# Residual adds by transfer, row-wise mixing of one column of weights, and a later statistic, at the start of the second layer of a deformable convolution and a mixture-of-experts convolution

## The chip, the core and the metric

The kernel runs on one core of one Trainium2 chip. A core has five engines that each work through their own queue in order: TensorE (PE; its weight loads are listed as PEld), VectorE (DVE), ScalarE (ACT), GpSimd (POOL) and SyncE (SP), which here only issues DMA transfers. POOL issues transfers too, from a queue of its own. All of them share 16 DMA engines. Matrix products go to PSUM, everything else lives in SBUF. The metric is the time of one execution on the device, in microseconds.

## What is computed

Two layers on eight images of 128 channels and 64 x 64 pixels, in float32. Both layers have a residual, and both normalise their input per group of four channels first. Cut to what matters here:

```python
# layer 0: deformable convolution, batch norm over all images, relu
y = deform_conv(group_norm(x), off_w, off_b, w, b)
x = x + relu((y - mean(y)) * rsqrt(var(y) + 1e-5) * gamma + beta)
# layer 1: mixture of four 3x3 convolutions, two chosen per image
g = group_norm(x)
scores = sigmoid(mean(g, (2, 3)) @ gate_w.T + gate_b)
wd = dense(top2(scores + gate_bias), scores)      # (8, 4), sums to 1 per image
x = x + sum_e wd[:, e] * conv3x3(g, expert_w[e]) + conv3x3(g, shared_w) + biases
```

The convolution is linear in its weights, so the kernel mixes the four experts and the shared weights into one set per image, and adds the residual as a multiple of the identity in the middle tap.

## The kernel before

`dense()` is layer 0: it samples, convolves and writes the raw result of each image to DRAM (`ydram`), with statistics for the batch norm. It ends at about 1043 us of the profile. `layer1()` then takes one image after another.

**Preparing an image** is a generator, `prepare(b, made)`. Its `yield`s are the places where it hands back control, and so set where its instructions land in each engine's queue. It has these steps:

1. Batch norm, relu and residual. For image 0 this goes over eight chunks `c` of 512 pixels per channel (lines 1410 to 1421): a relu on ACT (line 1415) in place in `x1`, an add of `xt0`, the input that was loaded ahead, by POOL for even chunks and by VectorE for odd ones (line 1417), and, two chunks later, the chunk's statistics on VectorE (`bn_stats`, line 1419). For the other images it goes over four quarters: a relu (line 1426) and a transfer from DRAM, issued by POOL, that adds the input onto `x1` as it lands (line 1429). Their statistics are on line 1437.
2. The group statistics: aggregate (line 1440), a small product with a grouping matrix for the mean (`pm`, line 1444), small operations on VectorE (`d`, `e`, `gm`), a second product for the variance (`pv`, line 1454), and a power on POOL (line 118) for the scale. For image 1 seven `yield`s stand ahead of `pm`, and one ahead of `pv`.
3. The gate: a product (`pg`, line 1476), a sigmoid, and a ranking on VectorE that gives the mixing weights `wd`. Between these ACT normalises the image into `pad2` in eight chunks (line 1467).
4. Mixing. `wmix` holds the mixed weights by row, column, output. Each of its columns `kx` is the shared weights plus four expert terms, one VectorE operation per expert (line 1546). From `wmix` come `u1` and `u2` (lines 1557 to 1561), since the convolution saves products by working on pairs of rows: product `j` is 0 with row 0 of the weights, 1 with `u1`, 2 with `u2`, 3 with row 2. `transform(g, which, engine)` (lines 1525 to 1529) makes the matching inputs `v` of block `g` from `pad2`: `which` 1 for product 1, `which` 2 for product 2, `which` 0 for products 0 and 3. For image 0 the three columns are mixed one after the other and the transforms of the first block stand between them; for the other images all columns are mixed at once.

**The products** of an image: four blocks `g` of 16 rows, in each the products `j` in the order 1, 2, 0, 3, in each three columns `kx` (line 1618). Only in image 0's first block does the loop over columns stand outside that over `j`, so that products can begin when column 0 is mixed. After each `j` a `collect` is put into the queues: ACT for `j` 1, VectorE for the others. Also after each `j`, the preparation of the next image goes on by two steps (three after `j` 3), and for image 0 its own remaining transforms by one.

**Transfers around the change.** SP's queue, in order: the last stores of layer 0, five small gate tensors, the shared weights `sw_sb` and the four experts' `ew_sb` (576 KB each, lines 1397 and 1399), image 1 (four of 512 KB, line 1379), then image 2 into the buffer of image 0 once that is normalised. Image 0 and its input are loaded while layer 0 still runs.

The instructions that only run under `tc.If` at the end of the program (a general form of layer 0, and layer 1 once more) do not run here.

Of the kernel before, what the change touches and what calls it, by code (L numbers as in the profile page):

```python
# [11 lines left out]
ALU = mybir.AluOpType  # L12
# [17 lines left out]
NE = 4  # L30
# [35 lines left out]
def deform_moe_conv(  # L66
# [18 lines left out]
    nc = tc.nc  # L85
# [10 lines left out]
        out=gsel, in_=gsel, compare_op=ALU.is_ge, fill=0.0, base=0,  # L96
# [3 lines left out]
        out=gsel, in_=gsel, compare_op=ALU.is_ge, fill=0.0, base=3,  # L100
# [1237 lines left out]
    def layer1():  # L1338
# [6 lines left out]
        with ExitStack() as st:  # L1345
# [59 lines left out]
            def prepare(b, made):  # L1405
# [4 lines left out]
                if b == 0:  # L1410
                    for c in range(NCH + 2):
                        if c < NCH:
                            part = slice(c * CH, (c + 1) * CH)
                            y = x1[:, part]
                            nc.scalar.activation(y, y, AF.Relu, bias=yshift, scale=yscale)
                            adder = nc.gpsimd if c % 2 == 0 else nc.vector
                            adder.tensor_tensor(y, y, xt0[:, part], ALU.add)
                        if c > 1:
                            nc.vector.bn_stats(
                                stats[:, c - 2, :], x1[:, (c - 2) * CH : (c - 1) * CH]  # L1420
                            )
                else:

                    for q in range(4):
                        part = slice(q * HW // 4, (q + 1) * HW // 4)
                        nc.scalar.activation(
                            x1[:, part], x1[:, part], AF.Relu, bias=yshift, scale=yscale
                        )
                        nc.gpsimd.dma_start(
                            out=x1[:, part], in_=x[b, :, part], accum_op=ALU.add  # L1430
                        )
                        if b > 1:
                            yield
                    if b > 1:
                        yield
                    for c in range(NCH):
                        nc.vector.bn_stats(stats[:, c, :], x1[:, c * CH : (c + 1) * CH])
                        yield
# [10 lines left out]
                nc.vector.scalar_tensor_tensor(ev, d, d, mv[:, 1:2], ALU.mult, ALU.add)  # L1449
                gm = small.tile([P, 1], F32, name="gm")  # L1450
                nc.vector.tensor_tensor(gm, mv[:, 0:1], d, ALU.subtract)
                yield
                pv = ps_s.tile([P, 4], F32, name="pv", tag="pss")
                nc.tensor.matmul(pv[:, 0:1], lhsT=gsel, rhs=ev, start=True, stop=True)
                yield
# [10 lines left out]
                def normalise(c):  # L1466
                    nc.scalar.activation(
                        pad2[:, 1 + 8 * c : 9 + 8 * c, 1 : W + 1],
                        x1[:, c * CH : (c + 1) * CH].rearrange("p (h w) -> p h w", w=W),
                        AF.Identity, bias=shift, scale=scale,  # L1470
                    )
# [48 lines left out]
                def transform(g, which, engine):  # L1520
                    v, r = vs[g], 2 * TR * g
                    even = pad2[:, r + 2 : r + 2 * TR + 2 : 2]
                    odd = pad2[:, r + 1 : r + 2 * TR + 1 : 2]
                    if which == 1:
                        engine.tensor_tensor(v[:, 2 * TR : 3 * TR], odd, even, ALU.add)  # L1525
                    elif which == 2:
                        engine.tensor_tensor(v[:, 3 * TR :], even, odd, ALU.subtract)
                    else:
                        engine.tensor_tensor(
                            v[:, 0 : 2 * TR], pad2[:, r : r + 2 * TR],  # L1530
                            pad2[:, r + 2 : r + 2 * TR + 2], ALU.subtract,
                        )
# [9 lines left out]

                for kx in range(3) if b == 0 else (slice(0, 3),):
                    part = wmix[:, :, kx]
                    for e in range(NE):
                        nc.vector.scalar_tensor_tensor(
                            part, experts[:, e, :, kx], wd[:, e : e + 1],
                            part if e else shared[:, :, kx], ALU.mult, ALU.add,
                        )
                        if b:  # L1550
                            normalise(4 + e)
                            yield
                    if b or kx == 1:
                        nc.vector.scalar_tensor_tensor(
                            wmix[:, 1, 1], ident, inv, wmix[:, 1, 1], ALU.mult, ALU.add
                        )
                    nc.vector.tensor_tensor(u2[:, kx], part[:, 0], part[:, 2], ALU.add)
                    nc.vector.tensor_tensor(u1[:, kx], u2[:, kx], part[:, 1], ALU.add)
                    if kx == 0:
                        transform(0, 1, nc.vector)  # L1560
                    nc.vector.tensor_tensor(u2[:, kx], u2[:, kx], part[:, 1], ALU.subtract)
                    if kx == 0:
                        transform(0, 2, nc.vector)
                        transform(0, 0, nc.vector)
                    yield
                if b == 0:
                    mix_biases()
# [16 lines left out]
            for b in range(B):  # L1584
                load(b + 2)
                ahead_of = prepare(b + 1, made) if b + 1 < B else iter(())
                vs, us, bmix = made.pop(b)
                for g in range(NG):
                    yo = b2.tile([P, TR, 2, W], F32, name="yo")
                    part = {}  # L1590

                    def collect(j, pc, g=g, b=b, yo=yo, part=part, bmix=bmix):

                        if j == 1:
                            part["t"] = b2.tile([P, TR, W], F32, name="t1")
                            nc.scalar.activation(part["t"], pc, AF.Identity, bias=bmix, scale=0.5)  # L1596
                        elif j == 2:
                            for name, sign in (("s", 0.5), ("d", -0.5)):
                                part[name] = b2.tile([P, TR, W], F32, name=name + "12")
                                nc.vector.scalar_tensor_tensor(  # L1600
                                    part[name], pc, sign, part["t"], ALU.mult, ALU.add
                                )
                        elif j == 0:
                            nc.vector.tensor_tensor(yo[:, :, 0], pc, part["s"], ALU.add)
                        else:
                            nc.vector.tensor_tensor(yo[:, :, 1], part["d"], pc, ALU.subtract)
                            n = 2 * TR * W
                            nc.sync.dma_start(
                                out=out[b, :, g * n : (g + 1) * n],
                                in_=yo.rearrange("p t i w -> p (t i w)"),  # L1610
                            )

                    def product(j, kx, pc):
                        rows = {
                            0: slice(0, 2 * TR, 2), 1: slice(2 * TR, 3 * TR),
                            2: slice(3 * TR, 4 * TR), 3: slice(1, 2 * TR, 2),
                        }[j]
                        nc.tensor.matmul(  # L1618
                            pc, lhsT=us[j][:, kx], rhs=vs[g][:, rows, kx : kx + W],
                            start=(kx == 0), stop=(kx == 2),  # L1620
                        )

                    order = (1, 2, 0, 3)
                    pcs = {}
                    if b == g == 0:

                        pcs = {j: ps_m.tile([P, TR, W], F32, name="pc") for j in order}
                        for kx in range(3):
                            for j in order:
                                product(j, kx, pcs[j])  # L1630
                    for j in order:
                        pc = pcs.get(j)
                        if pc is None:
                            pc = ps_m.tile([P, TR, W], F32, name="pc")
                            for kx in range(3):
                                product(j, kx, pc)
                        todo.append((collect, j, pc))
                        if len(todo) > 1:
                            f, *args = todo.pop(0)
                            f(*args)  # L1640
                        if b == 0:
                            next(first, None)
                        for _ in range(3 if j == 3 else 2):
                            next(ahead_of, None)
                for _ in ahead_of:
                    pass
# [59 lines left out]
```

## Time and profile before

| what | us |
|---|---|
| three runs | 1418.2, 1424.83, 1427.55; median 1424.83 |
| the profiled execution | 1419.31 |
| its span, first to last instruction | 1417.3 |
| TensorE busy in the span | 1290.2 (91%) |
| VectorE busy | 1063.5 (75%) |
| ScalarE busy | 834.3 (59%) |
| POOL busy | 477.6 (34%) |

The span by stage. The columns are the busy time of PE and of VectorE, the TensorE clock that was granted as a share of the full one, and what the DMA engines moved:

| stretch, us | what | PE | DVE | clock | GB/s |
|---|---|---|---|---|---|
| 0 to 50 | start of layer 0 | 17.59 | 30.58 | 0.86 | 120 |
| 50 to 1010 | layer 0 | 899.88 of 960 | 738.88 | 0.97 | 186 |
| 1010 to 1043 | end of layer 0 | 31.55 of 33 | 6.37 | 1.00 | 23 |
| 1043 to 1067 | batch norm, image 0 prepared | 1.99 of 24 | 17.26 | 0.58 | 259 |
| 1067 to 1113 | products of image 0, image 1 prepared | 43.67 of 46 | 41.28 | 0.96 | 121 |
| 1113 to 1417 | images 1 to 7 | 295.49 of 304 | 229.16 | 1.00 | 124 |

An engine's busy time matters in a stage where it is close to the stage's length. A wait is told with what released it: "[2.33 <-DVE e L1449]" behind an instruction says that its engine stood idle for 2.33 us until VectorE's operation of line 1449 had written `e`.

### The profile page before, as it was taken

How to read it: one execution, taken by the hardware profiler on the slowest of the kernel's cores; microseconds unless marked ns; L12 is line 12 of the kernel's file. 1: busy time of each engine (PE TensorE's matmuls, PEld its weight loads, DVE VectorE, ACT ScalarE, POOL GpSimd, SP SyncE). 2: the span in 40 equal slices, each digit the busy share in tenths (PEclk: the TensorE clock that was granted, in tenths of full speed). 3: DMA queues.
4: the chain of work that ended last, by engine and by line, in shares of the span. 5: the costliest groups of instructions: out<-in, count | busy, mean ns of one | idle time of the engine just before them, and what ended most of it. 6: DMA issues, size and time to landing. Idle time of an engine off the chain costs nothing.

```text
span 1417.3 us, 21259 instructions
## 1 busy us (share of the span) xinstructions
PE 1290.2 (91%) x7561; PEld 731.6 (52%) x7561; DVE 1063.5 (75%) x2124; ACT 834.3 (59%) x1110; POOL 477.6 (34%) x748
## 2 busy tenths in 40 slices
PE   4169889999999999999999999999948999999998
PEld 1144456555656655655565565666623444444443
DVE  5757868689788878968978886756448987778972
ACT  2365856886787688688679768767522333222220
POOL 6444044534425543452552554354021010001000
PEclk9579989999999999999999999999978999999999
DMA  4589686977978887897887887799245654456411
GB/s 145 114 192 206 137 182 157 213 182 171 210 181 180 194 195 175 180 207 184 193 210 183 179 207 159 159 228 220 66 160 147 163 146 123 127 153 178 104 57 51
DMA packets 149430, 234.55 MB, mean 165 GB/s; under 512 B 101677, under 2 KB 104890, under 8 KB 139074
## 3 DMA queue, kind: packets, MB, share of 16 engines
q0 software_dynamic: 79248, 136.19, 44.4%
q1 hardware_dynamic: 69522, 96.37, 24.2%
q8 instruction: 61, 1.00, 0.3%
q10 hardware_dynamic: 544, 0.54, 0.1%
q14 instruction: 55, 0.45, 0.1%
HBM read 180.23 MB, written 45.35 MB: 159 GB/s over the span
## 4 chain that ended last, share of the span: by engine, by line
PE 57%; DMA 12%; ACT 12%; issue 8%; DVE 6%; POOL 3%; SPq 2%; DVEq 0%; ACTq 0%; POOLq 0%
PE py L934 21%; PE pc L1618 17%; PE pq L884 11%; DMA ywts<-taby 3%; PE pc L456 3%; PE pt L825 3%; ACT xwts L776 2%; DMA combo<-colwise 2%; ACT work L638 2%; DMA pad<-in_x_dram 1%; ACT samples L894 1%; DMA x<-in_x_dram 1%; DVE s L868 1%; POOL ywts L738 1%; ACT xt L841 1%
## 5 line engine op out<-in xcount | busy, mean ns | idle before, releaser
L934 PE MATMUL py<-samples,dw_sb 128*128 128x512 f32 (+3 forms) x1296 | 555.1, 561 | 9.7 <-ACT y L942 9.7
L738 POOL DMA_DIRECT2D ywts<-taby x510 | 335.0, 671 | 368.0 <-DMA xwts<-tabx 151.8
L934 PEld LDWEIGHTS py<-samples,dw_sb 128*128 128x128 f32 x1296 | 226.8, 189 | 206.8 <-issue 174.2
L884 PE MATMUL pq<-s,xt 64*128 64x144 f32 (+1 forms) x3840 | 284.4, 302 | 29.8 <-ACT samples L894 22.5
L884 PEld LDWEIGHTS pq<-s,xt 64*128 64x128 f32 x3840 | 257.6, 191 | 78.6 <-ACT samples L894 26.9
L894 ACT COPY samples<-pq 128x864 f32<-128x864 f32 (+1 forms) x318 | 278.5, 973 | 27.2 <-PE pq L884 27.1
L868 DVE TENSOR_TENSOR s<-xwts,ywts 128x432 f32<-128x432 f32 (+1 forms) x448 | 199.0, 498 | 49.5 <-PE pq L884 45.4
L1618 PE MATMUL pc<-v,u 128*128 128x512 f32 x384 | 174.3, 600 | 6.3 <-DVE v L1525 6.3
L1618 PE MATMUL pc<-v,wmix 128*128 128x512 f32 x384 | 173.2, 596 | 0.0
L776 ACT ACTIVATE xwts<-xwts,place 128x1152 f32<-128x1152 f32 (+3 forms) x132 | 153.1, 1164 | 7.9 <-DMA xwts<-tabx 7.9
L782 DVE TENSOR_SCALAR xwts<-xwts 128x1152 f32<-128x1152 f32 (+2 forms) x128 | 96.0, 751 | 80.4 <-ACT xwts L776 75.3
L1596 ACT ACTIVATE t<-pc,bmix 128x512 f32<-128x512 f32 x32 | 22.0, 687 | 187.5 <-PE pc L1618 98.8
L757 POOL DMA_DIRECT2D xwts<-tabx x126 | 73.5, 590 | 164.3 <-DVE samples L911 34.9
L1618 PEld LDWEIGHTS pc<-v,u 128*128 128x128 f32 x384 | 71.8, 191 | 92.9 <-issue 83.1
L1618 PEld LDWEIGHTS pc<-v,wmix 128*128 128x128 f32 x384 | 72.0, 189 | 90.9 <-issue 88.9
L942 ACT ACTIVATE y<-py,db_sb 128x512 f32<-128x512 f32 (+3 forms) x72 | 45.8, 636 | 118.0 <-PE py L934 110.8
L828 ACT COPY xt<-pt 128x512 f32<-128x512 f32 x126 | 73.9, 587 | 61.0 <-PE pt L825 51.4
L825 PEld LDWEIGHTS pt<-ident,picked 128*128 128x128 f32 x504 | 59.0, 142 | 92.5 <-ACT xt L828 41.8
L825 PE MATMUL pt<-ident,picked 128*128 128x128 f32 x504 | 78.1, 278 | 23.5 <-DVE picked L791 17.0
L791 DVE COPY picked<-pad 128x512 f32<-128x512 f32 x128 | 71.9, 604 | 32.0 <-PE pt L825 31.9
L841 DVE COPY xt<-xt 32x896 f32<-32x896 f32 x126 | 77.7, 616 | 2.4 <-ACT xt L828 0.9
L1014 DVE BATCH_NORM_STATS2 ystats<-y 128x6 f32<-128x512 f32 (+3 forms) x72 | 44.2, 622 | 23.7 <-ACT y L942 23.7
(209 smaller groups left out, 1167.0 us busy)
## 6 DMA issues: line engine op xcount, KB each, us to landing
xwts<-tabx POOLq DMA_DIRECT2D x126, 576.0 KB, 8.5
pad<-in_x_dram SPq DMA_DIRECT2D x36, 512.0 KB
ywts<-taby POOLq DMA_DIRECT2D x126, 144.0 KB, 9.2
out_dram<-yo SPq DMA_DIRECT2D x32, 512.0 KB
ywts<-taby POOLq DMA_DIRECT2D x126, 108.0 KB, 8.9
yd<-y SPq DMA_DIRECT2D x48, 256.0 KB
ywts<-taby POOLq DMA_DIRECT2D x126, 72.0 KB, 8.3
pad<-yd SPq DMA_DIRECT2D x16, 512.0 KB
```

What stands on the lines that cost most here:

```text
L738: engine.dma_start(out=y_wts[g % 3][HALF * h + k : HALF * (h + n) : Q, first : last + 1].rearrange("p r a b c -> p (r a b c)"), in_=bass.A ...
L757: engine.dma_start(out=x_wts[g % 3][HALF * h : HALF * h + HALF], in_=bass.AP(tensor=x_table[b].tensor, offset=x_table[b].offset + (2 * j + ...
L776: nc.scalar.activation(some, some, AF.Abs, bias=columns[side])
L782: nc.vector.tensor_scalar(some, some, -1.0, 0.0, ALU.add, ALU.min)
L825: nc.tensor.transpose(pt[:, c - c0], one.rearrange("p h x y -> p (h x y)"), ident)
L828: (nc.vector.tensor_copy if turn_odd else nc.scalar.copy)(xts[g][:, c0 : c0 + n], pt[:, 0:n])
L841: move(out=xts[g][rows, EVEN:].rearrange("p c n -> p (c n)"), in_=xts[g][rows, 1 - side : EVEN - side].rearrange("p c n -> p (c n)"),)
L868: nc.vector.tensor_tensor(s[:, :, 3 * at : 3 * (at + k)].rearrange("p m (c x) -> p m c x", x=3), by_x[:, :, c : c + k], by_y[:, :, w : w + ...
L884: nc.tensor.matmul(by_m[:, h, :, at : at + k], lhsT=xts[g][rows, c // 2 + EVEN * (c % 2)], rhs=s[rows, :, at : at + k], start=True, stop=True,
L894: (nc.scalar.copy if g or q < 3 else nc.vector.tensor_copy)(bass.AP(tensor=one.tensor, offset=one.offset + first, ap=[list(one.ap[0]), [M ...
L934: nc.tensor.matmul(py, lhsT=dw_sb[:, 3 * (2 - yy) + 2 - xx], rhs=samples[g % 2][:, m : m + 3 * n - 2 : 3, xx, 1 : W + 1], start=(i == 0), ...
L1618: nc.tensor.matmul(pc, lhsT=us[j][:, kx], rhs=vs[g][:, rows, kx : kx + W], start=(kx == 0), stop=(kx == 2),)
```

## The change

Four edits, all in `layer1()`.

- The residual add of image 0: chunks 1, 3, 4 and 5 get it by an adding transfer from DRAM that POOL issues (256 KB each: 128 rows of 2 KB), as the other images have it by quarters. Chunks 0, 2, 6 and 7 are added by VectorE. POOL adds none.
- Image 1's second statistics product, `pv`, comes three steps later in the generator, and so does all of the image's preparation that follows it.
- Column 0 of image 0's weights is mixed row by row, in the order row 0, row 2, row 1: twelve operations of 128 elements per partition where there were four of 384. The transform for products 0 and 3 of the first block stands right behind row 0's mix; before, it stood behind the other two transforms.
- In the first block of image 0 the products of column 0 go in the order 0, 3, 1, 2. Columns 1 and 2 keep 1, 2, 0, 3.

```diff
                             nc.scalar.activation(y, y, AF.Relu, bias=yshift, scale=yscale)
-                            adder = nc.gpsimd if c % 2 == 0 else nc.vector
-                            adder.tensor_tensor(y, y, xt0[:, part], ALU.add)
+                            if c in (1, 3, 4, 5):
+                                nc.gpsimd.dma_start(
+                                    out=y, in_=x[b, :, part], accum_op=ALU.add
+                                )
+                            else:
+                                nc.vector.tensor_tensor(y, y, xt0[:, part], ALU.add)
...
-                yield
+                for _ in range(4 if b == 1 else 1):
+                    yield
                 pv = ps_s.tile([P, 4], F32, name="pv", tag="pss")
...
                     part = wmix[:, :, kx]
-                    for e in range(NE):
-                        nc.vector.scalar_tensor_tensor(
-                            part, experts[:, e, :, kx], wd[:, e : e + 1],
-                            part if e else shared[:, :, kx], ALU.mult, ALU.add,
-                        )
-                        if b:
-                            normalise(4 + e)
-                            yield
+                    soon = b == 0 and kx == 0
+                    for rows in (slice(0, 1), slice(2, 3), slice(1, 2)) if soon else (slice(0, 3),):
+                        for e in range(NE):
+                            nc.vector.scalar_tensor_tensor(
+                                part[:, rows], experts[:, e, rows, kx], wd[:, e : e + 1],
+                                part[:, rows] if e else shared[:, rows, kx], ALU.mult, ALU.add,
+                            )
+                            if b:
+                                normalise(4 + e)
+                                yield
+                        if soon and rows.start == 0:
+                            transform(0, 0, nc.vector)
...
                     if kx == 0:
                         transform(0, 2, nc.vector)
-                        transform(0, 0, nc.vector)
                     yield
...
                         for kx in range(3):
-                            for j in order:
+                            for j in order if kx else (0, 3, 1, 2):
                                 product(j, kx, pcs[j])
```

## The prediction

> **What bounds the kernel now.** I read the page's slices first (TensorE is 8 or 9 tenths busy from the fourth on, but for the 30th with 4), then the busy time by stretch around that hole, then the chain of waits through it, then the timeline, last the landings of the adding transfers. By stretch (us, then busy us and count on PE, PEld, DVE, ACT, POOL; granted clock; DMA share; GB/s):
>
> ```profile
> 1040.00:1060.00 20.00, 4.33 (x20) 3.40 (x18) 11.57 (x30) 6.50 (x10) 8.55 (x14) 0.67 0.62 227
> 1060.00:1080.00 20.00, 13.65 (x28) 5.98 (x29) 18.20 (x44) 10.89 (x14) 3.60 (x4) 0.74 0.92 234
> 1080.00:1122.00 42.00, 39.67 (x97) 17.72 (x96) 37.77 (x71) 13.11 (x17) 4.02 (x5) 1.00 0.43 122
> ```
>
> From 1043 to 1067 TensorE has next to nothing to do: what runs there is on the path, one to one. From 1067 to 1076 VectorE sets the pace (18.20 of 20 us busy), then TensorE. The chain (start, length, what) says what is in the hole:
>
> ```profile
> 1047.49 0.81 ACT pad L1415
> ...
> 1054.73 1.80 DVE stats L1419 x3
> 1056.56 0.38 DVE mv L1440
> ...
> 1062.96 0.63 DVE wmix L1546
> ...
> 1066.87 22.92 PE pc L1618 x48
> ```
>
> So: eight relus, adds and statistics to 1056.56; 6.4 us of small operations on the statistics; 3.9 us from the first mix of weights to the first product. The timeline (start, length, engine) gives the prices:
>
> ```profile
> 1046.77 5.75 ACT L1415 ACTIVATE pad<-pad,yshift,yscale 128x512 f32<-128x512 f32 x8 [3.14 <-DVE yshift L1344]
> 1048.03 1.99 SPq L1399 DMA_DIRECT2D ew_sb<-in_expert_w_dram  x4
> 1050.06 1.98 SPq L1379 DMA_DIRECT2D x<-yd  x4
> 1063.61 1.93 DVE L1546 SCALAR_TENSOR_TENSOR wmix<-ew_sb,wd,wmix 128x384 f32<-128x384 f32 x3
> 1071.33 0.35 DVE L1554 SCALAR_TENSOR_TENSOR wmix<-ident,inv,wmix 128x128 f32<-128x128 f32 x1
> 1072.26 0.30 PEld L1618 LDWEIGHTS pc<-v,u 128*128 128x128 f32 x2 [0.73 <-DVE u L1558]
> 1075.73 0.30 PEld L1618 LDWEIGHTS pc<-v,u 128*128 128x128 f32 x2 [0.59 <-DVE u L1558]
> 1092.24 0.38 PE L1454 MATMUL pv<-e,gsel 128*128 128x1 f32 x2 [2.33 <-DVE e L1449]
> 1113.04 0.19 PEld L1618 LDWEIGHTS pc<-v,u 128*128 128x128 f32 x1 [0.24 <-DVE v L1529]
> ```
>
> The reader is to see that SP issues the expert weights and image 1 just as the relus run, that columns 1 and 2 of the weights (1072.26, 1075.73) wait for VectorE, one stall of 2.33 us in image 0, and when image 1 begins (1113.04).
>
> **Adding transfers.** Half the adds move from POOL (chunks 0, 2, 4, 6) and VectorE (1, 3, 5, 7) to transfers for 1, 3, 4, 5; VectorE adds 0, 2, 6, 7. POOL's four adds and their 6.40 us go, and they cost nothing now: VectorE's statistics ended last. Added are four issues on POOL. The nearest row is the same instruction for later images, line 1429, 512 KB each, 0.86 us of POOL, starting 0.35 us after its relu. Relu 1 ends at 1047.49 + 0.81 = 1048.30, the others 0.70 apart, so the issues start at about 1048.65, 1050.05, 1051.0 and 1051.9 (the last two spaced by POOL). POOL's next work, the `pow` of line 118 (now 1058.94), is behind them, not late. Landing is the question. Issue to landing for image 1, and then for the first two of image 2:
>
> ```profile
> DMA to landing us min/median/max: 7.8/9.9/11.9
> DMA to landing us min/median/max: 9.9/11.3/12.6
> ```
>
> In the first set (issued from 1067.34, 1.13 us apart) landings follow each other after 1.13 + (11.9 - 7.8)/3 = 2.5 us; SP's queue had run dry at 1072. In the second, SP's queue was full: 1.12 + 2.7 = 3.8 us. The queues over 1118 to 1121 say why:
>
> ```profile
> q0 software_dynamic: 104, 0.42, 69.5%
> q1 hardware_dynamic: 104, 0.41, 35.9%
> ```
>
> Packet for packet, and an adding packet takes twice the engine time of a plain one. In the hole SP's queue holds 0.6 + 2.4 + 2.1 MB from 1048 and now moves near 400 GB/s until 1062, so all four meet it. A 256 KB transfer has the same 128 rows at half the length. Halving bytes gives 1.25 us per landing alone, 1.9 beside SP; with packets of 2 KB alternating against SP's of 4.6 KB it is 8 pairs an engine of about 0.165 + 0.165 us (half of 104 x 4 KB at 69.5% of 48 engine-us, or 0.32 us; 4.6 KB at 400 GB/s over 16 engines, 0.18), about 2.8. I take 2.4. The first lands 7.8 - 1.25 = 6.55 to 9.9 - 1.9 = 8.0 us after issue, at 1055.2 to 1056.65; I take 1055.9. The fourth: 1055.9 + 3 x 2.4 = 1063.1, between 1055.2 + 3 x 1.25 = 1059.0 and 1056.65 + 3 x 2.9 = 1065.4.
>
> VectorE is in order: statistics 1 wait for the first transfer with adds 6 and 7 queued behind; harmless, since statistics 5 wait for the last, and 5, 6, 7 (1.80 us) and the aggregate follow. The aggregate moves from 1056.56 to 1063.1 + 1.9 = 1065.0: **+8.4 us** (+4.3 to +10.7), and everything up to the mix moves with it. The four transfers slow SP's queue: weights land some 6 us later, but are used 8.4 later; image 1 too, whose relu (1065.8) also moves.
>
> A rule is weighed here. The Trainium skill, "DMA: Bandwidth & Descriptors", section "Anatomy of one DMA — SWDGE (gpsimd) path", gives a transfer from POOL 2.0 us plus its bytes over 436 GB/s: 2.6 us for 256 KB. The fourth would land at 1051.9 + 2.6 = 1054.5 and the aggregate would be at 1056.4, -0.2 us. The rows show no adding transfer under 6.2 us (the minimum of all 28 of line 1429). The trace decides: this stretch has the full queue that the fit leaves out.
>
> **Mix row by row.** For column 0, four operations of 384 elements (0.655 us apart) become twelve of 128. The nearest row is line 1554, 0.35 us; dependent ones follow 0.03 later (384: 0.62 becomes 0.655), independent ones 0.08 earlier, so 9 x 0.38 + 3 x 0.27 = 4.23 against 2.62: **+1.6 us** of VectorE (bounds 0 and, at 0.40 each, +2.2). The transforms and sums are the same, in another order. Counted from the first mix, the first product can start at 4 x 0.36 + 1.25 = 2.7 us instead of 3.9; product 3 next; then product 1 at 6.7 and product 2 at 7.5. That gains nothing: columns 1 and 2 wait for VectorE already (0.73 and 0.59 us), and VectorE begins column 1 at 7.4 instead of 5.76. TensorE then idles some 2.4 us ahead of column 1. So the whole +1.6 is on the path.
>
> A second rule: "TensorE: Matmul & The Clock Gate", "Part 1: The HAM clock gate", lets the clock rise after about 3.4 us of work and fall after an idle window as long. The trace agrees with the rise: the first four records take 0.89 us each, and 0.43 from 1070.44, 3.6 us after the first. By the rule an idle 2.4 us does not drop it: 0. If it does drop, column 1's eight records at 0.89 take 7.1 us where VectorE's spacing is 3.47: +3.6.
>
> **The variance product of image 1, three steps later.** It leaves the place where TensorE waits 2.33 us and stands behind two products of the third block; the gate's product goes one further. TensorE is then up to 2.33 us ahead. Behind it VectorE has to take two more collects (2 x 0.65 us) before image 1's u and v. By the queues: `pv` at about 1095.3, VectorE waits for it 1.3 us; score at 1098.8, weights mixed by 1108.0, collects to 1109.3, u to 1111.4, v to 1112.1; TensorE gets there at 1111.3. Image 1's first product runs at 1112.4 against 1113.5 (its weights load at 1113.04): **-1.1 us** (-2.3 if VectorE keeps up, +1.5 if three steps, 3.9 us, come through less the stall removed).
>
> **Sum.** +8.4 + 1.6 - 1.1 = +8.9 us. The profiled execution took 1419.31 us (span 1417.3), 5.5 below the median of the three runs, 1424.83. On it the sum gives 1428.2; on the median **1433.7**, put at 1434.
>
> **Rivals.** (1) Not slower: the transfers land as the rule says, by 1054.5. Aggregate -0.2, +1.6 for the mix, -2.3 with the stall gone: -0.9, 1424. It decides where the fourth landing is before 1055. For it: POOL's issue path is idle and rows are few. Against: 6.2 us is the least seen. (2) Starved: 2 KB adding packets cost as much as 4 KB ones, so landings follow after 3.8 us and the first comes at 1056.65: 1068.05, aggregate +13.4, sum +13.9, 1439. For it: packets alternate one for one whatever their size. Against: time per byte dominates in plain packets. (3) The clock drops ahead of column 1: +8.9 + 3.6 = +12.5, 1437. For it: the granted clock is 0.67 and 0.74 here. Against: the idle time is short. That POOL doesn't issue these transfers is excluded by the order of instructions, which has four there.
>
> **Numbers.** Forecast 0.60, rival 1 0.14, rival 2 0.12, rival 3 0.14. The landing bounds give +4.3 + 1.6 - 2.3 = +3.6 to +10.7 + 1.6 + 1.5 = +13.8, that is 1428 to 1439; the before runs scatter by 7 us below and 3 above their median, so 1425 to 1441 leaves out a tenth at each end, mostly rivals 1 and 2. A measurement of this kernel can tell about 1% (14.2 us) from no change. Faster by that: 0.02, since even rival 1 gains 0.9. Slower by that: most of half of rival 2, a third of rival 3 and a twentieth of the forecast, 0.15. Within: 0.83.
>
> **What would show it.** Statistics of chunks 1, 3, 4, 5 waiting for transfers, the last landing at 1059 to 1065; aggregate 8 us later; column 1's first u 17.3 us after the aggregate (15.7 now); no stall at `pv`, and image 1 starting a microsecond sooner after column 2 than now. It is wrong if the fourth transfer lands before 1057, or if TensorE stalls over 3 us at image 1.

## The result, and the profile after

The changed kernel takes 1431.84 us (median of 14 runs, 1428.21 to 1435.81) where the kernel before, on the same chip, takes 1421.76 (14 runs). The ratio is 1.0069, 95% interval 1.0055 to 1.0084: slower by 10 us. The forecast was +8.9 us, nearly all of it (+8.4) from the transfers.

By stretch, cut at the last product of layer 0, the first product of image 0 and that of image 1 (columns as in the prediction):

```profile
1044.30:1077.60 33.30, 1.73 (x6) 1.50 (x6) 15.50 (x47) 11.97 (x18) 5.94 (x14) 0.55 0.70 212
1077.60:1125.00 47.40, 44.80 (x102) 19.07 (x102) 43.36 (x93) 15.79 (x20) 5.78 (x7) 0.95 0.57 154
1125.00:1428.80 303.80, 295.13 (x708) 130.23 (x708) 229.76 (x426) 79.39 (x104) 22.52 (x28) 1.00 0.43 119
```

The hole in TensorE's work has grown from 24 to 33 us, and nobody works more in it: VectorE is busy 15.50 us. Images 1 to 7 take 304 us as before. So the whole answer lies ahead of image 1. The timeline of the changed kernel, from the issues to the aggregate:

```profile
1049.76 0.97 POOL L1417 DMA_DIRECT2D pad<-in_x_dram  x1 [1.45 <-ACT pad L1415]
1051.17 2.65 POOL L1417 DMA_DIRECT2D pad<-in_x_dram  x3 [0.44 <-ACT pad L1415]
...
1058.55 1.29 DVE L1423 BATCH_NORM_STATS2 stats<-pad 128x6 f32<-128x512 f32 x2 [7.06 <-DMA pad<-in_x_dram]
1061.31 0.69 DVE L1423 BATCH_NORM_STATS2 stats<-pad 128x6 f32<-128x512 f32 x1 [1.47 <-DMA pad<-in_x_dram]
...
1063.94 0.69 DVE L1423 BATCH_NORM_STATS2 stats<-pad 128x6 f32<-128x512 f32 x1 [1.35 <-DMA pad<-in_x_dram]
...
1066.56 1.88 DVE L1423 BATCH_NORM_STATS2 stats<-pad 128x6 f32<-128x512 f32 x3 [1.34 <-DMA pad<-in_x_dram]
1068.47 0.37 DVE L1444 BATCH_NORM_AGGREGATE mv<-stats 128x2 f32<-128x48 f32 x1
```

In brackets are VectorE's waits for the four transfers: 7.06 + 1.47 + 1.35 + 1.34 = 11.2 us. The kernel before has no such wait here. Then column 0 of the weights and the start of column 1, TensorE and VectorE:

```profile
1074.89 0.35 DVE L1553 SCALAR_TENSOR_TENSOR wmix<-ew_sb,wd,sw_sb 128x128 f32<-128x128 f32 x1
...
1077.63 3.78 PE L1626 MATMUL pc<-v,wmix 128*128 128x512 f32 x4 [5.17 <-DVE v L1534]
...
1082.31 0.61 DVE L1553 SCALAR_TENSOR_TENSOR wmix<-ew_sb,wd,sw_sb 128x384 f32<-128x384 f32 x1
...
1085.85 1.98 PE L1626 MATMUL pc<-v,u 128*128 128x512 f32 x4 [2.08 <-DVE u L1567]
```

The first product comes 1077.63 - 1074.89 = 2.74 us after the first mix (3.91 before), column 1 begins on VectorE after 7.42 (5.76 before), and TensorE waits 2.08 us for it. Last, the moved product `pv` and image 1:

```profile
1103.21 0.28 PE L1448 MATMUL pm<-mv,gsel 128*128 128x1 f32 x2
1103.35 5.40 PE L1626 MATMUL pc<-v,u 128*128 128x512 f32 x12
1108.58 0.28 PE L1459 MATMUL pv<-e,gsel 128*128 128x1 f32 x2
...
1108.89 0.16 DVE L117 TENSOR_SCALAR ve<-pv 128x1 f32<-128x1 f32 x1 [1.30 <-PE pv L1459]
...
1125.15 5.42 PE L1626 MATMUL pc<-v,u 128*128 128x512 f32 x12 [0.43 <-DVE v L1530]
```

No stall at `pv`, the wait is VectorE's now (1.30), and 0.43 us come back at image 1.

Every profile can be divided at the same instructions, from image 0's first relu on, which leaves out the differences of a microsecond or two that layer 0 has from one execution to the next. Lengths in us, each the difference of two starts in the timeline, one profile per kernel (the kernels other than the first two are told below):

| kernel | first relu to aggregate | to first mix | to column 1's first product | to image 1's | to image 2's | to the end | sum |
|---|---|---|---|---|---|---|---|
| before | 9.79 | 6.40 | 9.30 | 41.20 | 43.04 | 260.76 | 370.5 |
| changed | 20.54 | 6.42 | 10.96 | 39.30 | 42.86 | 260.74 | 380.8 |
| transfers alone | 20.35 | 6.42 | 9.30 | 41.20 | 42.03 | 261.41 | 380.7 |
| mix alone | 9.78 | 6.39 | 10.96 | 42.90 | 42.43 | 260.67 | 373.1 |
| `pv` alone, 3 steps | 9.78 | 6.39 | 9.44 | 39.17 | 42.86 | 261.13 | 368.8 |
| mix and `pv` | 9.79 | 6.39 | 10.95 | 39.30 | 42.87 | 260.56 | 369.9 |
| one transfer | 16.03 | 6.42 | 9.68 | 40.82 | 42.61 | 261.52 | 377.1 |
| `pv` alone, 2 steps | 9.78 | 6.40 | 9.37 | 39.13 | 42.87 | 260.96 | 368.5 |
| transfers, SP held back | 13.77 | 6.41 | 9.38 | 44.24 | 42.59 | 261.42 | 377.8 |

Changed against before: +10.75 up to the aggregate (the transfers), +1.66 up to column 1 (the mix) and -1.90 up to image 1 (`pv`), together +10.5 of the sum's +10.3. That is the measured 10 us.

### The profile page after: what moved, and what is told of

Read it like the earlier page. It is cut to its first block, busy times and chain, and to the rows that moved or that the text cites. A ratio compares the mean times of both kernels' runs of the same rounds, so it can differ in the third digit from the quotient of the medians.

```text
span 1428.8 us, 21261 instructions
## 1 busy us (share of the span) xinstructions
PE 1291.4 (90%) x7561; PEld 732.7 (51%) x7561; DVE 1065.0 (75%) x2132; ACT 836.3 (59%) x1110; POOL 473.9 (33%) x748
```

## The experiments

The three parts were run one by one, then two of them together, then the price of the transfers was taken apart. All are edits of the kernel before.

**Transfers alone.**

```diff
-                            adder = nc.gpsimd if c % 2 == 0 else nc.vector
-                            adder.tensor_tensor(y, y, xt0[:, part], ALU.add)
+                            if c in (1, 3, 4, 5):
+                                nc.gpsimd.dma_start(out=y, in_=x[b, :, part], accum_op=ALU.add)
+                            else:
+                                nc.vector.tensor_tensor(y, y, xt0[:, part], ALU.add)
```

> Only the adding transfers, all else as before. If the three parts add up: the aggregate of the statistics comes 10 to 11 us later, and the time grows by 10.7 us (ratio 1.0075), a little more than the whole change. If the transfers were mostly hidden and the row-wise mix or the later variance product carried the loss: under 5 us (ratio under 1.0035).

Measured: ratio 1.0090, interval 1.0068 to 1.0113; the aggregate comes 20.35 - 9.79 = 10.6 us later. The transfers carry the loss; the interval holds the expected 1.0075.

**Row-wise mix alone** (the edits of lines 1546 to 1563 and of the products' order).

> Only the row-wise mix of column 0 and the order 0, 3, 1, 2. VectorE's path theory: VectorE begins column 1 at 7.4 us after the first mix instead of 5.8, TensorE waits 2 us more ahead of column 1, time +1.7 us (ratio 1.0012). Rival, the earlier first product pays: TensorE's start 1.2 us sooner reaches the end, time -1.2 us (0.9992). Rival, the clock drops in the gap ahead of column 1: +5 us (1.0036).

Measured: ratio 1.0024, interval 1.0014 to 1.0035, or 2 to 5 us. Column 1 comes 1.66 us later, as VectorE's path says, and the rival by which the earlier product pays is out. A clock that falls ahead of column 1 is out too: this profile grants 1.00 there, and 1.0036 lies just outside the interval. The remainder was not expected: in this profile image 0 takes another 42.90 - 41.20 = 1.70 us. TensorE of this kernel at the statistics of image 1, and the stretches there:

```profile
1089.94 0.28 PE L1444 MATMUL pm<-mv,gsel 128*128 128x1 f32 x2
1092.55 0.38 PE L1454 MATMUL pv<-e,gsel 128*128 128x1 f32 x2 [2.33 <-DVE e L1449]
1092.80 7.09 PE L1621 MATMUL pc<-v,u 128*128 128x512 f32 x12
```

```profile
1089.00:1092.90 3.90, 1.57 (x8) 0.92 (x7) 3.87 (x10) 0.00 (x0) 0.00 (x0) 1.00 0.29 119
1092.90:1096.30 3.40, 3.40 (x6) 1.33 (x6) 1.80 (x6) 0.00 (x0) 0.56 (x1) 0.50 0.37 154
1096.30:1100.00 3.70, 3.70 (x12) 1.78 (x11) 0.00 (x0) 1.39 (x2) 0.00 (x0) 1.00 0.00 0
```

The same twelve records that take 5.40 us in the kernel before (at 1092.48 there) take 7.09: the clock fell to 0.50 for 3.4 us after the 2.33 us stall at `pv`. The stall is as long in the kernel before, whose profile shows no fall. What differs is where it lies. In all nine profiles every stretch between two changes of the clock lasts a whole number of beats of 3.41 us. Cut at the beats, the stall of the mix alone lies inside one of them, the last before the fall:

```profile
1089.49:1092.90 3.41, 1.08 (x7) 0.73 (x6) 3.38 (x9) 0.00 (x0) 0.00 (x0) 1.00 0.18 76
```

In the kernel before it is spread over two, and TensorE is busy for over 2 us in each:

```profile
1087.57:1090.98 3.41, 2.33 (x8) 1.02 (x6) 3.41 (x6) 0.00 (x0) 0.00 (x0) 1.00 0.37 154
1090.98:1094.39 3.41, 2.15 (x7) 1.20 (x8) 3.07 (x8) 0.00 (x0) 0.22 (x1) 1.00 0.20 85
```

Over the nine profiles the clock fell 63 times, always after a beat with at most 1.44 us of TensorE's work; the 3371 beats at full clock with 1.50 us or more had no fall behind them.

So the remainder is probably a price of the mix and the stall together. The mix moves the stall 1.66 us later against image 0's first relu, near which a beat begins in all nine profiles (within 0.35 us), and so into one beat. A fall in every run would make 1.66 + 1.70 = 3.4 us, a ratio of 1.0024, which is what the 22 runs gave. Their mean granted clock agrees: 0.9663 against 0.9676 for the 43 runs before, 0.0013 less, give or take 0.0009 (95%), where one fall makes 0.0012. The fall itself is seen in the one profile alone.

**The later `pv` alone.**

```diff
-                yield
+                for _ in range(4 if b == 1 else 1):
+                    yield
                 pv = ps_s.tile([P, 4], F32, name="pv", tag="pss")
```

> Only image 1's variance product three steps later. Theory: the 2.33 us stall of TensorE goes, 0.4 us of it come back at image 1's first product, time -1.9 us (ratio 0.9987), faster than both kernels. Rival, the stall only moves to image 1's start because VectorE is full there: 0 (1.0000). Rival, image 1's weights come late: +1.5 us (1.0011).

Measured: ratio 0.9994, interval 0.9984 to 1.0004. Its profile says -2.03 us up to image 1, with 0.42 us left there. The interval of the time holds both -1.9 us and none; late weights, +1.5, are out.

**Mix and `pv` together**, adds as before.

> The row-wise mix and the later variance product together, adds as before: the whole change without its transfers. Theory of the stages (1.7 us lost ahead of column 1, 1.9 us won at the variance product, each as in its own trace): ratio 0.9998. Rival, the mix costs more than its 1.7 us in most executions, because its gaps leave TensorE's clock at half for longer: as alone, 1.0024 less the gain of the other part, so 1.001 to 1.002.

Measured: ratio 1.0006, interval 0.9992 to 1.0019. The stages are those of the two parts (10.95 and 39.30, sum -0.6 us), and the clock shows no fall now that the stall is gone. The interval takes in both expectations, so a price of the mix beyond its 1.66 us is, in this kernel, neither shown nor excluded.

**Transfers with SP held back.** The transfers alone, but SP's large loads are moved behind the statistics of chunk 5, and one small copy holds them until those are done:

```diff
-                (sw_sb, shared_w),
             ):
                 nc.sync.dma_start(out=t, in_=src)
-            for e in range(NE):
-                nc.sync.dma_start(out=ew_sb[:, e], in_=expert_w[:, e])
-            load(1)
...
+                        if c == 7:
+                            nc.vector.tensor_copy(sw_sb[:, 0, 0:1], stats[:, 5, 0:1])
+                            nc.sync.dma_start(out=sw_sb, in_=shared_w)
+                            for e in range(NE):
+                                nc.sync.dma_start(out=ew_sb[:, e], in_=expert_w[:, e])
+                            load(1)
```

> Only the adding transfers, with SP's loads of the weights and of image 1 held back until the last of them has landed. Contention theory: the first lands 5.5 to 6.5 us after its issue, the others 1.3 to 1.5 us apart, statistics of the last chunk 6 us sooner than with the loads beside them. Rival, a transfer of 128 rows has a price of its own whatever else moves: 8.8 us and 2.6 us apart as in the changed kernel. The time is not to be read as a gain: the weights and image 1 arrive late.

Measured, issue to landing of the four, first in the changed kernel, then here:

```profile
DMA to landing us min/median/max: 8.8/11.1/14.0
```

```profile
DMA to landing us min/median/max: 4.0/5.8/6.9
```

And VectorE here, at each of them, up to the aggregate:

```profile
1054.65 1.29 DVE L1419 BATCH_NORM_STATS2 stats<-pad 128x6 f32<-128x512 f32 x2 [2.25 <-DMA pad<-in_x_dram]
1057.27 0.69 DVE L1419 BATCH_NORM_STATS2 stats<-pad 128x6 f32<-128x512 f32 x1 [1.33 <-DMA pad<-in_x_dram]
...
1059.15 0.69 DVE L1419 BATCH_NORM_STATS2 stats<-pad 128x6 f32<-128x512 f32 x1 [0.60 <-DMA pad<-in_x_dram]
...
1060.44 0.69 DVE L1419 BATCH_NORM_STATS2 stats<-pad 128x6 f32<-128x512 f32 x1
...
1062.62 0.37 DVE L1446 BATCH_NORM_AGGREGATE mv<-stats 128x2 f32<-128x48 f32 x1
```

The first lands after 4.0 us, sooner than the 5.5 to 6.5 expected, and the last no longer makes VectorE wait. The next two let VectorE start 2.62 and 1.88 us after the one before, which is more than the 1.3 to 1.5 expected; the changed kernel has 2.76 and 2.63 there. The relus begin at 1048.85 here, so the aggregate stands at +13.8 us: 6.6 us sooner than beside the loads, still 4.0 later than with plain adds. Contention with SP's loads is five eighths of the transfers' price; the other three are there on an idle queue. The rival with a fixed price is out. All this is one run. Its time, 1428.4 us, is not read, but not for the reason expected: the weights come in time (6.41 and 9.38 us to the first mix and to column 1, as elsewhere), and image 1 does not (ACT waits 1.2 us for its load, VectorE 1.2 us for its adding transfers). TensorE stands at `pv` for 3.68 us, which fills nearly a whole beat, and the clock falls here too:

```profile
1099.72 0.43 PE L1460 MATMUL pv<-e,gsel 128*128 128x1 f32 x2 [3.68 <-DVE e L1455]
```

```profile
1096.51:1099.92 3.41, 0.20 (x2) 0.20 (x2) 3.38 (x9) 0.00 (x0) 0.00 (x0) 1.00 0.23 96
1099.92:1103.34 3.42, 3.42 (x6) 1.59 (x6) 1.96 (x6) 0.00 (x0) 0.56 (x1) 0.50 0.37 153
```

**One transfer**, for chunk 1; the other adds stay on POOL and VectorE.

```diff
-                            adder = nc.gpsimd if c % 2 == 0 else nc.vector
-                            adder.tensor_tensor(y, y, xt0[:, part], ALU.add)
+                            if c == 1:
+                                nc.gpsimd.dma_start(out=y, in_=x[b, :, part], accum_op=ALU.add)
+                            else:
+                                adder = nc.gpsimd if c % 2 == 0 else nc.vector
+                                adder.tensor_tensor(y, y, xt0[:, part], ALU.add)
```

> One adding transfer alone, for chunk 1; the other adds on POOL and VectorE as before. Latency theory: it lands 8 to 9 us after its issue beside SP's loads, VectorE stands before statistics 1 and then has 5.5 us of adds and statistics left, so the aggregate is 6 us later, ratio 1.0045. Rival, what counts is the 2.6 us that each transfer takes from the queue: 2.6 us later, 1.0018. Rival, one transfer hides: 1.000.

Measured: ratio 1.0063, interval 1.0042 to 1.0085, which holds the expected 1.0045; the aggregate comes 6.24 us later. Its VectorE around the landing:

```profile
1056.96 1.29 DVE L1424 BATCH_NORM_STATS2 stats<-pad 128x6 f32<-128x512 f32 x2 [3.16 <-DMA pad<-in_x_dram]
...
1060.54 1.87 DVE L1424 BATCH_NORM_STATS2 stats<-pad 128x6 f32<-128x512 f32 x3
1062.45 0.37 DVE L1445 BATCH_NORM_AGGREGATE mv<-stats 128x2 f32<-128x48 f32 x1
```

From 1056.96 to 1062.45 are the 5.5 us of adds and statistics that queue behind statistics 1. A quarter of the transfers costs three fifths of the delay (6.24 of 10.6 us): it is the first landing that hurts most, and the order of VectorE's queue that passes it on. A price of 2.6 us per transfer is out as the measure, and so is a hidden transfer.

**Two steps instead of three for `pv`** (the range above with 3 in place of 4).

> Image 1's variance product two steps later instead of three, all else as before. If image 1's first product is what gives 0.4 us back with three steps, two steps save the same stall and give nothing back: 0.9983. If VectorE is late at the variance product with two steps still: part of the 2.33 us stays, 0.9990 to 1.0000.

Measured: ratio 0.9984, interval 0.9971 to 0.9997, faster than both kernels. The number is as expected, the reason is not: image 1 still waits 0.33 us, and its stage is that of three steps (39.13 against 39.17 us). That two steps are better than three is not shown, since the intervals overlap. That the stall at `pv` was worth removing is shown by the two steps; three alone are not clear of no change.

## Why the prediction was right

The direction, the cause and the order of the three terms came out; the time lies in the range. That it lies within 2 us of the forecast is in part luck. The base of three runs, 1424.83, is 3.1 us above the median of 14, and the rise was forecast 1.2 us too small. Within the rise two misses offset each other: the transfers cost 2.3 us more than forecast, and the variance product gave 0.8 us more. Term by term:

- *Adding transfers*, +8.4 forecast (+4.3 to +10.7): +10.75 in the changed kernel, +10.6 alone. This is the term that was mis-sized most, at its upper bound. Two estimates made it up. The first landing after issue, taken as 7.25 us between 6.55 and 8.0, was 8.76. Two things probably made it short: the middle took in a row (7.8) beside which SP's queue had run dry, and the bytes saved were deducted from a delay of which half or more, 4.4 of 8.8 us here, passes before the first packet (last section). No run separates them. The spacing, taken as 2.4 as a middle of 1.9 by bytes and 2.8 by packets, was (14.0 - 8.8 + 2.8)/3 = 2.7, where 2.8 is the time from the first to the last issue. So the fourth landed at 1066.5, or 1065.4 counted from the first relu as it stood before, at the edge of the 1059 to 1065 named as a sign. The account by packets was right, and nearer than it was written down: eight pairs of 0.165 + 0.165 us are 2.64, not 2.8. The queues of the changed kernel over 1055 to 1065:

```profile
q1 hardware_dynamic: 525, 2.04, 54.7%
q0 software_dynamic: 523, 0.97, 52.8%
```

  523 adding packets against 525 of SP's, one for one; the adding ones move 0.97 MB in 10 us, which is one transfer of 256 KB in 2.7 us. A middle between two accounts should not have been taken where one of them had its mechanism in a row.
- *The page's 2.6 us a transfer* against the trace's rows: the trace was right to decide. On the idle queue the first landing took 4.0 us and the last 6.9, so even without SP's loads the fit is short here.
- *Mix row by row*, +1.6: +1.66, and VectorE begins column 1 at 7.42 us (7.4 forecast), the first product at 2.74 (2.7). TensorE waits 2.08 us ahead of it; the clock did not fall there in any profile. But the reason given, that an idle time shorter than about 3.4 us does not drop it, does not hold: the 2.33 us at `pv` dropped it in the mix alone. Ahead of column 1 the beat with the gap had 1.58 to 1.78 us of work in the three kernels with the mix, little above the 1.44 after which the clock still fell. The 0 came out narrowly, not by the rule.
- *The variance product*, -1.1 (-2.3 to +1.5): -1.90. VectorE's wait at `pv` is the forecast 1.30 us. The queues behind it were followed to 1.1 us of waiting at image 1 (TensorE there at 1111.3, its product at 1112.4), where 0.43 were left.
- *Rivals.* Landing by the page is out by the 14.0 us of the fourth. Starved at 3.8 us apart is out by 2.7. A falling clock was named at the wrong place: ahead of column 1 it did not fall, at the stall of `pv` it did in two profiles, the mix alone and the transfers with SP held back.

## What to carry to other kernels

Where a transfer takes over an add, price it by its landing beside whatever the queues hold at that moment: here the wait for the first packet, and then packet for packet. A consumer that works in order passes the wait on to all that is queued behind it. Work that is moved ahead on TensorE gains nothing when the operation behind it still waits for VectorE, and every instruction that the split adds to VectorE is then paid in full. A short product that waits in TensorE's queue is worth moving behind the next product or two. A short stall may cost clock too, and whether it does seems to depend on where it lies: in the mix alone a shift of 1.66 us probably brought it on.

## What the runs showed of the hardware

- TensorE's clock changes on a beat of 3.41 us, and a beat in which TensorE is idle in part can drop it: in all nine profiles it fell after beats with at most 1.44 us of work and never after those with 1.50 or more. So the 2.33 us stall with two short statistics products around it dropped the clock for 3.4 us in one profile (the mix alone) and not in two others (before, and transfers alone). That the place in the beat decides is read from these profiles; no run moved the stall alone. The Trainium skill, "TensorE: Matmul & The Clock Gate", "Part 1: The HAM clock gate", asks for an idle window of about 3.4 us; the length of the fall agrees with such a window, the idle time that was enough does not.
- The adding transfers wait long for their first packet when SP's queue is full. In the changed kernel none ran from 1049.8, where the first was issued, to 1054.2:

```profile
DMA packets 354, 1.34 MB, mean 305 GB/s; under 512 B 63, under 2 KB 63, under 8 KB 354
## 3 DMA queue, kind: packets, MB, share of 16 engines
q1 hardware_dynamic: 354, 1.34, 92.7%
```

  With SP held back none ran for 1.6 us after the issue (1050.7 to 1052.3), and then they had the engines to themselves (1052.4 to 1053.4):

```profile
q0 software_dynamic: 76, 0.16, 98.0%
```

  So most of the 4.8 us between a first landing after 4.0 and one after 8.8 us passes before the first packet (4.4 us or more against 1.6).
